# The low half of a split gelu: a VectorE subtraction, or a TensorE product and a ScalarE copy

## The chip, the cores and the metric

The kernel runs on one core of a Trainium2 chip. The metric is the device time of one execution in microseconds (us); the times shown are medians of several executions. A profile is one execution taken by the hardware profiler, and its times are counted from the first instruction of the span.

## What is computed

The input x is 8 batches of 512 tokens of width 256. Four blocks follow one another, each added to x: attention A (16 heads, attention within each token over the 64 channels of a head), a feed-forward block, attention B (causal, over the 512 tokens), and the same feed-forward block again. The part that the change touches is the feed-forward block, FFN for short:

```
def _L0_ffn_ref(x, w1_w, w1_s, w2_w, w2_s, h1_w, h1_s, h2_w, h2_s, w3_w, w3_s):
    def _tlin(x, w, s):
        return jnp.einsum('bsi,oi->bso', x, w) * s
    h = jax.nn.silu(_tlin(x, w1_w, w1_s)) * _tlin(x, w2_w, w2_s)
    h = jax.nn.gelu(_tlin(h, h1_w, h1_s), approximate=False)
    h = jax.nn.gelu(_tlin(h, h2_w, h2_s), approximate=False)
    return _tlin(h, w3_w, w3_s)
...
x = x + _L0_attn_a_ref(_layernorm(x, axis=-1), ...)
x = x + _L0_ffn_ref(_layernorm(x, axis=-1), ...)
x = x + _L0_attn_b_ref(_layernorm(x, axis=-1), ...)
x = x + _L0_ffn_ref(_layernorm(x, axis=-1), ...)
```

The hidden width is 1024, and w1, w2, h1, h2 and w3 are ternary (-1, 0, 1) with a scale for each output. The layers h1 and h2 are called the first and the second inner layer here.

## The kernel before

The kernel has two halves that run at the same time. One is attention A, in the class `AttentionA`: 8 batches, 4 groups of heads, 4 tiles of 128 tokens, 4 units of scores each. The other is the generator `after_a`: for each batch whose attention A is done, the FFN, attention B and the FFN again. So while attention A works on batch b+1, the rest of batch b runs beside it. A loop at the end of `fast_path` weaves the two by hand: each step of attention A is given out in three parts, and after each part the generator is advanced until the budget it yields (`yield 0.225 * len(step)` and so on, 309.5 a batch) has caught up. The engines' programs are then in the order in which the Python code issued them[...]. Nothing is reordered by a scheduler: an instruction that waits holds up all that stands behind it on its engine.

Attention A of one group needs all engines: TensorE projects q, k and v (L761, L766), ScalarE copies k (L781, L782), GpSimd and VectorE multiply the scores (L804), ScalarE takes the exponentials (L818), VectorE multiplies them by v (L828), a DMA that GpSimd issues adds one half of the tile to the other (L834), GpSimd folds it once more (L839), VectorE sums the rows (L865), and GpSimd adds the sums up (L872). After the last batch's attention A only the generator is left.

In the FFN, TensorE multiplies with float32r operands. Since these are rounded, an activation h is kept as two tiles: `h(0, m)`, the rounded value, and `h(1, m)`, what the rounding lost; `m` counts the 8 blocks of 128 hidden units. Each product is made twice, once with each half, and summed in PSUM. The first inner layer makes its two halves so: TensorE makes the product `pj` (L1140, one PSUM bank of 128 x 512); ScalarE writes gelu of it, rounded, to `h(0, m)` (L1105), and once more, not rounded, back over `pj` in PSUM (L1107); VectorE writes `pj - h(0, m)`, rounded, to `h(1, m)` (L1111).

The second inner layer keeps only one full float32 value, so L1107 and L1111 run for the first layer alone: 8 of each in each of the 16 FFNs.

When each of these is issued is set by the list `pending`: `later(fn)` puts a function there, and `flush()` runs and empties what the list held when it was called. The inner layers go over pairs of blocks, `m0` = 0, 2, 4, 6. The 32 products of a pair are issued in four steps of eight (three steps of 12, 12 and 8 for `m0` = 0), with a flush after each step but the last. The gelus of a pair are put on the list when its last step is out; they are issued at the flush after the first step of the next pair, and what they put on the list (`low`) at the flush after that pair's second step. The PSUM pool `ps_f` that holds `pj` has five buffers, and so a pair's bank comes free when `low` has read it.

Of the kernel before, what the change touches and what calls it, by code (L numbers as in the profile page):

```python
# [10 lines left out]
F32R = mybir.dt.float32r  # L11
BF16 = mybir.dt.bfloat16
AF = mybir.ActivationFunctionType
ALU = mybir.AluOpType
AX = mybir.AxisListType

P = 128
# [267 lines left out]
def fast_path(ctx: ExitStack, tc: tile.TileContext, k, t, flag):  # L285

    nc = tc.nc
    ident = k.ident

    const = ctx.enter_context(tc.tile_pool(name="const", bufs=1))  # L290
# [206 lines left out]
    for x1 in xn1:  # L497
        nc.gpsimd.memset(x1, 1.0)
    turn = [0]


    bank = ps_a.tile([P, 2, GW], F32, name="bank")
# [412 lines left out]
    def later(fn):  # L915
        pending.append(fn)
# [98 lines left out]
    def chunks(name):  # L1015


        pairs = {}

        def part(p, m):  # L1020
            if m // 2 not in pairs:
                pairs[m // 2] = block(f"{name}_{m // 2}", F32R).rearrange("p (n m s) -> p n m s", n=2, m=2)
            return pairs[m // 2][:, p, m % 2]

        return part
# [8 lines left out]
    def ffn(u, b, xt, nx, after):  # L1034
# [8 lines left out]
        h = chunks(f"h0_{u}")  # L1043
# [58 lines left out]
        def gelus(layer, ms, pss, h):  # L1102
            for m, pj in zip(ms, pss):
                scale = s_sb[:, 2 + layer, m : m + 1]
                nc.scalar.activation(h(0, m), pj, AF.Gelu, scale=scale)  # L1105
                if layer == 0:
                    nc.scalar.activation(pj, pj, AF.Gelu, scale=scale)  # L1107

            def low():
                for m, pj in zip(ms, pss):  # L1110
                    nc.vector.tensor_tensor(h(1, m), pj, h(0, m), ALU.subtract)  # L1111

            if layer == 0:
                later(low)

        for layer in range(2):
            h_in = h
            if layer == 0:
                h = chunks(f"h1_{u}")
            else:  # L1120
                h2 = [block(f"h2_{u}_{j}") for j in range(2)]
                h = lambda p, m: h2[m // 4][:, m % 4 * S :][:, :S]
            for m0 in range(0, MC, 2):
# [6 lines left out]
                pss = [ps_f.tile([P, S], F32, tag="pf", name=f"ph{layer}_{u}_{m}") for m in (m0, m0 + 1)]  # L1130
# [7 lines left out]
                for n, step in enumerate(steps):  # L1138
                    for j, p, c in step:
# [4 lines left out]
                            start=(p == 0 and c == 0),  # L1144
                            stop=(p == 1 and c == MC - 1),
# [5 lines left out]
                    if n < len(steps) - 1 or m0 < MC - 2:  # L1151
                        yield 0.225 * len(step)
                later(lambda layer=layer, m0=m0, pss=pss, h=h: gelus(layer, (m0, m0 + 1), pss, h))
            yield 2
            flush()
# [224 lines left out]
@with_exitstack  # L1380
def hybrid_kernel(ctx: ExitStack, tc: tile.TileContext, t):

    nc = tc.nc
    shared = ctx.enter_context(tc.tile_pool(name="shared", bufs=1))
    ident = shared.tile([P, P], F32, name="ident")
    make_identity(nc, ident)
    one = shared.tile([P, 1], F32, name="one")
    nc.gpsimd.memset(one, 1.0)
    eps = shared.tile([P, 1], F32, name="eps")
    nc.gpsimd.memset(eps, EPS)  # L1390
    power = shared.tile([P, NT], F32, name="power")
    nc.gpsimd.memset(power, -0.5)
    flag = shared.tile([P, 1], mybir.dt.int32, name="flag")

    ident16 = shared.tile([P, P], BF16, name="ident16")
    nc.vector.tensor_copy(ident16, ident)
    tmask16 = shared.tile([P, P], BF16, name="tmask16")
    nc.gpsimd.memset(tmask16, 0.0)
    nc.gpsimd.affine_select(tmask16, tmask16, [[1, P]], ALU.is_ge, NEG, base=0, channel_multiplier=-1)
    k = SimpleNamespace(ident=ident, one=one, eps=eps, power=power, ident16=ident16, tmask16=tmask16)  # L1400
    fast_path(tc, k, t, flag)
    with tc.If(nc.values_load(flag[0:1, 0:1], min_val=0, max_val=1) > 0):
        general_path(tc, k, t)
# [68 lines left out]
```

## Time and profile before

| | |
|---|---|
| time, median of 3 runs | 3989.1 us (3984.17 to 3989.51) |
| span of the profiled execution | 3990.8 us |
| mean granted TensorE clock | 0.849 |
| attention A alone (nothing beside it) | to 489 us |
| attention A beside FFNs and attention B | 489 to about 3665 us |
| last batch's FFN, attention B, FFN, alone | about 3665 to 3991 us |
| first inner layer, one pass beside attention A (14 of them) | 41.6 to 46.5 us |
| first inner layer, one pass alone (2 of them) | 29.0 us |

The span is the time from the first to the last instruction of one core. It is 1.7 us above the median of the timed runs; the profile's own sums are made against the span, and a difference found in them is taken off the median.

In the lines of the views, PE is TensorE, PEld its weight loads, DVE VectorE, ACT ScalarE, POOL GpSimd and SP the engine that issues most of the DMAs. `L1111` is a line of the kernel before. An engine's busy time doesn't count the time in which it issues a DMA, which matters for GpSimd.

### The profile page before, as it was taken

Reading aid. Unit: us, or ns where it says so; the run is one execution under the profiler, and the core shown is the slowest. Engines: PE = TensorE matmul, PEld = TensorE weight load, DVE = VectorE, ACT = ScalarE, POOL = GpSimd, SP = SyncE. Lnnn points to the kernel's source line nnn. Section 1 sums busy time; section 2 is a strip of 40 time slices with the busy share of each in tenths; the row PEclk is TensorE's granted clock in tenths of the full one; section 3 lists DMA queues with packets and bytes.
Section 4 is the critical chain, followed back from the end, with each engine's and each line's share of the span. In section 5 each row is a group of like instructions: output and inputs, shape, how many; then the busy total and the mean of one; then the engine's idle time right before and its main releaser. Section 6 shows DMA issues by size and latency. Waiting matters only on the chain.

```text
span 3990.8 us, 37932 instructions
## 1 busy us (share of the span) xinstructions
PE 3039.9 (76%) x12464; PEld 2055.2 (52%) x12464; DVE 3375.9 (85%) x3776; ACT 2341.3 (59%) x3156; POOL 3077.9 (77%) x3040
## 2 busy tenths in 40 slices
PE   5653487687877878678876878778787778778988
PEld 2231264365634656356643656346553556446847
DVE  7999988998899888998899988998989888996115
ACT  3444475576665675666755766666755767565342
POOL 6888878887888788887788887887888877886111
PEclk7556599798987988888987989879898889879999
DMA  8766777577776877768775877668776677767304
GB/s 229 182 137 137 159 197 158 124 191 189 199 154 139 196 191 178 148 163 202 200 157 118 208 186 194 149 142 213 174 190 143 160 182 206 158 129 211 116 28 169
DMA packets 118346, 669.24 MB, mean 168 GB/s; under 512 B 12662, under 2 KB 31865, under 8 KB 43643
## 3 DMA queue, kind: packets, MB, share of 16 engines
q0 software_dynamic: 78336, 570.46, 63.2%
q1 hardware_dynamic: 39804, 96.27, 6.7%
q8 instruction: 101, 1.65, 0.2%
q14 instruction: 105, 0.86, 0.1%
HBM read 254.07 MB, written 9.96 MB: 66 GB/s over the span
## 4 chain that ended last, share of the span: by engine, by line
DVE 38%; PE 18%; POOL 14%; DMA 13%; ACT 8%; issue 8%; SPq 0%; ACTq 0%; POOLq 0%; DVEq 0%
DVE red L865 15%; DMA w<-w 13%; DVE w L828 10%; PE ph L1140 5%; ACT w L818 4%; POOL w L804 3%; POOL w L839 3%; DVE ws L828 3%; PE pqkb L1187 3%; POOL acc L872 3%; DVE w L804 2%; DVE ws L804 2%; POOL h L1056 2%; POOL w L834 2%; DVE acc L876 2%
## 5 line engine op out<-in xcount | busy, mean ns | idle before, releaser
L818 ACT ACTIVATE w<-w 128x2048 f32<-128x2048 f32 x384 | 733.8, 1912 | 659.2 <-POOL w L804 461.3
L1140 PE MATMUL ph<-h,hidden 128*128 128x512 f32 x4096 | 1042.9, 411 | 72.4 <-POOL h L1056 42.9
L804 POOL TENSOR_TENSOR w<-k 128x1024 f32<-128x1024 f32 x512 | 1077.4, 2104 | 7.7 <-ACT k L782 7.1
L1140 PEld LDWEIGHTS ph<-h,hidden 128*128 128x128 f32 x4096 | 792.3, 195 | 275.3 <-POOL h L1056 53.8
L828 DVE TENSOR_TENSOR w<-w,qv 128x1024 f32<-128x1024 f32 x768 | 898.8, 1211 | 22.4 <-ACT w L818 22.4
L865 DVE TENSOR_REDUCE red<-w 128x128 f32<-128x1024 f32 (+1 forms) x384 | 601.3, 1566 | 178.0 <-DMA w<-w 93.6
L839 POOL TENSOR_TENSOR w<-w 128x1024 f32<-128x1024 f32 x256 | 643.7, 2514 | 82.9 <-DMA w<-w 82.3
L834 POOL DMA_DIRECT2D w<-w x384 | 337.9, 880 | 349.0 <-issue 121.1
L872 POOL TENSOR_TENSOR acc<-acc,red 128x256 f32<-128x256 f32 (+1 forms) x640 | 471.2, 736 | 142.7 <-DVE red L865 122.0
L865 DVE TENSOR_REDUCE red<-ws 128x256 f32<-128x2048 f32 (+1 forms) x256 | 435.4, 1742 | 0.0
L766 PE MATMUL qv<-wqv,xnta 128*128 128x512 f32 x512 | 299.7, 716 | 104.6 <-DVE ws L828 95.4
L1072 PE MATMUL pw<-xnt,gate 128*128 128x512 f32 (+2 forms) x1152 | 301.8, 422 | 21.7 <-ACT silu L1048 16.1
L828 DVE TENSOR_TENSOR ws<-ws,qv 128x1024 f32<-128x1024 f32 (+3 forms) x512 | 294.3, 635 | 27.6 <-ACT ws L818 27.6
L804 DVE TENSOR_TENSOR w<-qv,k 128x1024 f32<-128x1024 f32 x256 | 301.1, 1218 | 3.6
L804 DVE TENSOR_TENSOR ws<-qv,k 128x1024 f32<-128x1024 f32 (+3 forms) x512 | 299.5, 646 | 0.2 <-issue 0.2
L888 PE MATMUL bank<-ident,acc 128*128 128x128 f32 x256 | 62.4, 333 | 284.5 <-ACT k L781 278.6
L818 ACT ACTIVATE ws<-ws 128x1920 f32<-128x1920 f32 x128 | 231.5, 1808 | 80.7 <-DVE ws L804 80.1
L1072 PEld LDWEIGHTS pw<-xnt,gate 128*128 128x128 f32 x1152 | 230.8, 215 | 76.2 <-ACT silu L1048 20.4
L1249 ACT ACTIVATE eb<-psb 128x256 f32<-128x256 f32 (+3 forms) x512 | 182.1, 443 | 139.1 <-PE psb L1246 138.6
L1166 PE MATMUL pof<-w,h 128*128 128x256 f32 x1024 | 244.9, 392 | 22.8 <-ACT h L1105 22.8
L1105 ACT ACTIVATE h<-ph,s_sb 128x512 fp32r<-128x512 f32 (+1 forms) x256 | 171.2, 688 | 151.1 <-PE ph L1140 149.7
L876 DVE RECIPROCAL acc<-acc 128x256 f32<-128x256 f32 x128 | 222.9, 1741 | 11.9 <-POOL acc L872 11.9
(149 smaller groups left out, 4846.4 us busy)
## 6 DMA issues: line engine op xcount, KB each, us to landing
w<-w POOLq DMA_DIRECT2D x384, 1024.0 KB, 7.8
hidden<-in_h POOLq DMA_DIRECT2D x128, 1024.0 KB, 7.9
gate<-in_w12p POOLq DMA_DIRECT2D x32, 1024.0 KB, 9.1
w<-w_d SPq DMA_DIRECT2D x16, 1024.0 KB, 11.5
wqv<-wqv_d SPq DMA_DIRECT2D x31, 512.0 KB, 4.6
wo<-in_wo SPq DMA_DIRECT2D x32, 256.0 KB, 7.6
wbqk<-wbqk_d SPq DMA_DIRECT2D x8, 1024.0 KB, 9.0
w<-in_h SPq DMA_DIRECT2D x8, 1024.0 KB, 8.6
```

The lines of the kernel that those rows point to most:

```text
L766: nc.tensor.matmul(qv.rearrange("p j f -> p (j f)"), xnt[:, c, :], wqv[:, c, :], start=(c == 0), stop=(c == DC - 1),)
L804: eng.tensor_tensor(e, rows(q).to_broadcast(shape), columns(kt[:, 0]).to_broadcast(shape), ALU.mult)
L818: nc.scalar.activation(e, e, AF.Exp, scale=C**-0.5)
L828: nc.vector.tensor_tensor(ev, e, columns(qv[:, 1]).to_broadcast(list(e.shape)), ALU.mult)
L834: nc.gpsimd.dma_start(w[:, :2048], w[:, 2048:], accum_op=ALU.add)
L839: nc.gpsimd.tensor_tensor(w[:, :1024], w[:, :1024], w[:, 1024:2048], ALU.add)
L865: nc.vector.tensor_reduce(red, self.columns_of(w, n, off, nsq), AX.X, ALU.add)
L872: nc.gpsimd.tensor_tensor(rows, rows, part.rearrange("p a (x i) -> p a x i", i=n), ALU.add)
L876: nc.vector.reciprocal(acc[:, 0, :], acc[:, 0, :])
L1072: nc.tensor.matmul(pj[:, toks], w[:, m % 4, j, c, :], xs[:, p, c, toks], start=(p == 0 and c == 0), stop=(p == 1 and c == DC - 1),)
L1140: nc.tensor.matmul(pss[j], w[:, j, c, :], h_in(p, c), start=(p == 0 and c == 0), stop=(p == 1 and c == MC - 1),)
L1166: nc.tensor.matmul(po, h(0, c)[:, i * P : (i + 1) * P], w3[:, c, :], start=(c == 0), stop=False)
```

## The change

A constant tile `minus` is added: the 128 x 128 identity times -1, in float32r, made once by GpSimd. Where `low` subtracted on VectorE, a new function `less_high` now multiplies `h(0, m)` by `minus` on TensorE and adds the product onto `pj` in PSUM, so that the bank holds gelu minus its rounded copy. One flush later, ScalarE copies the bank, rounded, to `h(1, m)`. So the difference is issued on TensorE where it was on VectorE, and the tile `h(1, m)` is written one flush later, by ScalarE. The bank `pj` comes free after that copy.

```diff
--- before.py
+++ after.py
@@ -497,6 +497,8 @@
     for x1 in xn1:
         nc.gpsimd.memset(x1, 1.0)
     turn = [0]
+    minus = const.tile([P, P], F32R, name="minus")
+    nc.gpsimd.tensor_scalar(minus, ident, -1.0, None, ALU.mult)
 
 
     bank = ps_a.tile([P, 2, GW], F32, name="bank")
@@ -1106,12 +1108,17 @@
                 if layer == 0:
                     nc.scalar.activation(pj, pj, AF.Gelu, scale=scale)
 
+            def less_high():
+                for m, pj in zip(ms, pss):
+                    nc.tensor.matmul(pj, minus, h(0, m), start=False, stop=True, skip_group_check=True)
+                later(low)
+
             def low():
                 for m, pj in zip(ms, pss):
-                    nc.vector.tensor_tensor(h(1, m), pj, h(0, m), ALU.subtract)
+                    nc.scalar.copy(h(1, m), pj)
 
             if layer == 0:
-                later(low)
+                later(less_high)
 
         for layer in range(2):
             h_in = h
```

## The prediction

> **What bounds the kernel now.** I read the page's first part and chain first, then the windows of single stages, then the groups by form, and last the chain and the timeline inside two stages.
>
> ```profile
> PE 3039.9 (76%) x12464; PEld 2055.2 (52%) x12464; DVE 3375.9 (85%) x3776; ACT 2341.3 (59%) x3156; POOL 3077.9 (77%) x3040
> ...
> DVE 38%; PE 18%; POOL 14%; DMA 13%; ACT 8%; issue 8%; SPq 0%; ACTq 0%; POOLq 0%; DVEq 0%
> ```
>
> VectorE is the fullest engine and leads the chain, which speaks for taking work off it. But the change acts only in the first inner layer, so its stages decide:
>
> ```profile
> 1129.00:1223.00 94.00, 66.41 (x401) 29.25 (x399) 90.52 (x94) 60.58 (x109) 81.14 (x71) 0.88 0.70 150
> 1754.00:1799.00 45.00, 40.87 (x163) 31.30 (x162) 42.20 (x48) 37.60 (x44) 40.69 (x38) 0.94 0.86 207
> 2836.00:2879.00 43.00, 38.17 (x155) 29.78 (x155) 38.71 (x44) 34.78 (x39) 36.75 (x33) 0.96 0.84 200
> 3724.00:3753.00 29.00, 29.00 (x129) 24.02 (x128) 4.90 (x7) 10.96 (x18) 4.76 (x7) 1.00 0.43 145
> ```
>
> These are windows: length, then busy time of PE, PEld, DVE, ACT and POOL. The first is attention B beside attention A: DVE is full at 96%, the others have room. The next two are first inner layers beside attention A (a second and a first FFN of a batch): there PE, DVE and POOL are all busy for 85 to 94% of the window, and ACT has 7 to 8 us left. The fourth is one alone, all PE.
>
> The operation that goes, and its neighbours (busy time, mean ns, idle before and its releaser):
>
> ```profile
> L1055 ACT CAST h<-silu 128x512 fp32r<-128x512 f32 x128 | 78.6, 615 | 20.3 <-DVE silu L1051 19.9
> L1107 ACT ACTIVATE ph<-ph,s_sb 128x512 f32<-128x512 f32 x128 | 84.4, 659 | 0.0
> L1111 DVE TENSOR_TENSOR h<-ph,h 128x512 fp32r<-128x512 f32 x128 | 82.8, 676 | 40.0 <-ACT ph L1107 39.9
> ```
>
> The chain inside one second FFN's stage, start, length, what:
>
> ```profile
> 2696.79 0.68 DVE h L1111
> 2697.47 2.27 DVE w L804 x2
> 2699.74 0.02 issue
> 2699.77 1.92 ACT w L818
> 2701.70 1.28 ACT L1105
> ...
> 2706.03 1.50 DVE red L865 x2
> ...
> 2713.37 11.36 DMA w<-w
> ```
>
> It crosses four engines within 20 us, and L1111 holds about 1.7 us of it in a stage. Added up over the whole chain, L1111 stands there with 18 us in 49 pieces: of its 83 us, the rest lies beside other work.
>
> **What the Trainium skill says.** "TensorE: Matmul & The Clock Gate", section on the array's sub-arrays: ScalarE and VectorE are strict FIFOs. The trace agrees: L1111 sat 40 us at the head of DVE's queue until a gelu came. The same page has a warm 512-column matmul follow the last by about 216 ns; here 256 of L1140 take 58.03 us in the last stretch, 227 ns each. "ScalarE: Activation LUTs", section What ACT_TABLE_LOAD costs: 186 + 0.833 ns an element, so 612 ns for the copy, neighbours overlapping by 93; L1055 took 615, and two of them 1.12 us. Its section on table sets has copy in every set: no table load is added. "PSUM — Partial Sum Buffer", The four PSUM rules: only TensorE changes the has_written bits, so a product over a bank that ScalarE rewrote still adds to it. No run shows this yet.
>
> **The change part by part.** The built program has 128 instructions less on DVE, 128 more on PE, 128 more on ACT and one more on POOL.
>
> *Removed from DVE*: 8 x 0.676 = 5.4 us a stage. What is late next differs by stage.
> - Second FFNs beside attention A (7). At 2696 the first pair of L1111 goes, DVE's scores L804 end 1.28 us earlier, and ACT's exponential (idle 1.15 us for them) could start earlier; but two new copies, 1.12 us, now stand before it: nothing. At 2704 two L1111 and 1.2 us of waiting for gelus go, but the reduction after them needs POOL's fold L839, which ends at 2705.61: 0.4 us. At 2729 two L1111 of 1.28 us go from the chain between the landed DMA and the next issue: 1.25. In all 1.65 us, x 7 = 11.5.
> - The first FFNs of batches 0, 1 and 2 (3). The chain is POOL's up to the DMA and then passes L1111 once for 1.28 to 1.3: 3.9.
> - The first FFNs of batches 3 to 6 (4). PE runs without a gap from the late `h` of the gates, then hands to ACT:
>
> ```profile
> 2848.21 4.38 PE ph L1140 x11
> ...
> 2868.48 1.86 PE ph L1140 x8
> ...
> 2870.95 0.65 ACT ph L1107
> ...
> 2872.92 1.82 ACT ws L818
> 2874.74 0.03 issue
> 2874.76 2.35 DVE ws L828 x4
> ```
>
> Two pairs of added matmuls stand in that run, 4 x 0.227 = 0.9, with latency 1.0; at 2882.74 the chain loses 1.28 of L1111. Net 0.3 off, x 4 = 1.2.
>
> *Added to PE*: 8 x 0.227 = 1.8 us a stage. Beside attention A it lies in PE's gaps except in the four runs just counted. In the two stages of the last batch PE is at 100% (the window at 3724), so it counts whole: 2 x 1.8 = 3.6 us.
>
> *The new waits.* The added matmul waits for two gelus, with the next step's products and attention A's projections behind it on PE. Gelus are issued one step of eight (1.8 to 2.7 us) ahead of it; at 2696 they end 1.8 us before PE gets there, at 2706 2.5 us. In the first FFNs ACT itself waits for PE (2.35 us before L1105 at 2870), so PE can't overtake it. I take zero. The copy waits for the matmul, with attention A's exponentials behind it; it too is one step late, and I take its waiting as covered by ACT's idle time. The second pair is the tightest: PE would reach its matmul near 2708.4, ACT would be held from 2706.7, and the exponential at 2710.37 start 0.5 us later; its user on DVE (L828) starts only at 2715.00.
>
> *Added to ACT*: 8 copies, 4.5 us a stage, against 7 to 8 us idle. If no pair is covered, 14 x 4 x 1.12 = 63 us come on; the lower bound is zero, since ACT's gap is larger than the work. No price below zero: ACT loses nothing.
>
> *PSUM and start.* A bank is held one step longer. The second tile of the pair after next needs it, three steps later: 24 matmuls, over 5.4 us, against a copy of 1.1. Zero; if the copy is that late, PE stops. `minus` is one small POOL operation at the start, where POOL's next work waits for DVE up to 61 us: zero, at most 1 us.
>
> Sum: -11.5 - 3.9 - 1.2 + 3.6 = -13.0 us. Off the median, 3989.1 - 13.0 = 3976. The span is 1.7 us above that median, so the profile should show about 3978.
>
> **The rivals.**
> - *ScalarE becomes the late one (slower).* Each pair of copies not covered pushes the exponentials by 1.12 us, and DVE's L828 behind them. For it: 84% busy in the window at 1754, 94% with the copies, and a ring PE to ACT to PE to ACT in strict queues. Against: exponentials are mostly ready before DVE takes them. With half of the 56 pairs uncovered, 31 us against L1111's 18 and with PE's 3.6: +17, 4006. It decides from (18 - 3.6) / 1.12 = 13 pairs of 56.
> - *Hidden anyway (no change).* POOL was idle for 4.1 us before its DMA issues between 2679 and 2724, and for little else; the DMA takes 11 us whenever it starts. If POOL and the DMA take back all but a third of the gains, 5.5 off and 3.6 on: 3987.
> - *VectorE was the bound of the stage (more).* Each of the 14 shrinks until PE is full: 40.87 + 1.8 of 45 is 2.3, 38.17 + 1.8 of 43 is 3.0; mean 2.6, x 14 = 36, less 3.6: 3956. Against: POOL in the same windows.
> - That it doesn't do what it says: the counts of the program exclude it.
>
> **How the numbers follow.** Two results within 0.2% (8 us) can't be told apart here. The forecast, 3976, gets 0.46, of which 0.02 lies above 3981; more gain 0.10; hidden 0.22; slower 0.22. So faster 0.54, same 0.24, slower 0.22. The range goes from beyond the greatest gain, 3952, to the slower rival at half cover, 4004; about 2 in 10 are left out, mostly above.
>
> **What would show it.** L1111 is gone; a ScalarE row of 128 copies near 610 ns; a TensorE row of 128 matmuls. Right, if the idle time before these matmuls is small and not by ACT, if second FFNs' stages are 1 to 2 us shorter and the last stages 30.8 instead of 29.0. Wrong, if DVE's wait for ACT's L818 (50 us for w and ws before) grows by tens of us, if ACT waits long for the added matmul, or if the stages shrink by 2.5 us or more.

## The result and the profile after

The changed kernel takes 3995.1 us (median of 20 runs) against 3989.7 us of the kernel before (20 runs beside it): ratio 1.0012, interval 1.0005 to 1.0018. It is about 5 us slower, less than the 8 us that the prediction took as the least difference to be told apart; 3976 was forecast. The two profiled executions stand the other way round, 3989.3 us after and 3990.8 before. A single execution lies anywhere in a spread of some 10 us, so the traces are compared by stage and by wait here, and totals come from the timed runs.

First the page's busy times and the engines' shares of the chain, of the kernel after:

```profile
PE 3053.3 (77%) x12592; PEld 2072.2 (52%) x12592; DVE 3302.0 (83%) x3648; ACT 2400.9 (60%) x3284; POOL 3075.2 (77%) x3041
...
DVE 33%; PE 19%; POOL 17%; DMA 13%; ACT 9%; issue 8%; SPq 0%; POOLq 0%; ACTq 0%; DVEq 0%
```

VectorE gave up 73.9 us of busy time (3375.9 before) and the kernel is not faster for it. The new operations, from the groups by form (busy time, mean ns, idle before and its releaser):

```profile
L1118 ACT CAST h<-ph 128x512 fp32r<-128x512 f32 x128 | 68.4, 588 | 32.9 <-PE ph L1113 32.8
...
L1113 PE MATMUL ph<-h,minus 128*128 128x512 f32 x128 | 41.4, 397 | 3.8 <-ACT ph L1109 3.8
```

The copy costs 588 ns, close to the 612 put in, and no table load is added: ScalarE has 317 of them before and after. The matmuls' 397 ns overlap the matmuls around them (128 of them are busy for 41.4 us); what one adds is seen in the stage below.

Where the 73.9 us went is read in VectorE's waits (us in total, times, longest). The kernel before:

```profile
DVE red L865 <- DMA w<-w: 93.6, 40, 5.3
DVE red L865 <- POOL w L839: 84.1, 34, 5.7
...
DVE st L543 <- ACT x L1159: 41.1, 4, 31.3
DVE h L1111 <- ACT ph L1107: 39.9, 29, 7.3
DVE ws L828 <- ACT ws L818: 27.6, 15, 2.4
...
DVE w L828 <- ACT w L818: 22.4, 18, 2.9
```

The kernel after (its lines are 2 further down here):

```profile
DVE red L867 <- DMA w<-w: 118.0, 43, 6.2
DVE red L867 <- POOL w L841: 107.1, 50, 5.5
...
DVE st L545 <- ACT x L1166: 72.8, 4, 63.3
...
DVE ws L830 <- ACT ws L820: 47.8, 25, 4.7
DVE w L830 <- ACT w L820: 28.4, 25, 2.9
```

The row sums now wait 225.1 us for a tile that isn't there yet, 47.4 more; the products behind the exponentials wait 76.2, 26.2 more. Since the span is all but the same, the work that VectorE gave up must come back as waiting; over all rows the waits grew by about 72 us (594.9 to 666.4), and the rows show where. That these two changes make 73.6 us, almost the 73.9 us of work, is chance: the 39.9 us for L1111's gelus are gone too, and in the last batch L543 waits 31.7 us more.

The windows of the stages that the prediction showed (length, busy PE, PEld, DVE, ACT, POOL; then the granted clock), kernel after:

```profile
1751.00:1796.20 45.20, 41.69 (x170) 32.26 (x168) 38.38 (x42) 40.27 (x50) 40.72 (x38) 0.94 0.86 206
2832.80:2877.30 44.50, 39.69 (x163) 30.78 (x161) 36.40 (x39) 37.18 (x45) 37.36 (x34) 0.96 0.84 201
3718.20:3748.60 30.40, 30.40 (x135) 25.17 (x135) 0.75 (x1) 14.01 (x24) 4.79 (x7) 1.00 0.42 139
```

VectorE works 2.3 to 3.8 us less than before in the first two, and they are not shorter: 45.2 against 44.8 us and 44.5 against 43.2 from first matmul to the next stage's. GpSimd is at 40.72 of 45.20 us, where it was before. The third is the first inner layer alone: 1.4 us longer.

Over all stages, each taken from its first matmul to the first of the next (single profiled executions):

| stages | before | after | e1 |
|---|---|---|---|
| first inner layer beside attention A, 14 | 620.1 | 617.0 | 610.9 |
| second inner layer beside attention A, 13 | 574.3 | 590.1 | 593.3 |
| last layer of the FFN beside attention A, 13 | 483.4 | 467.7 | 466.6 |
| first inner layer alone, 2 | 58.0 | 60.8 | 58.0 |
| second inner layer alone, 2 | 58.0 | 59.0 | 58.0 |

The fourteenth second layer, in which attention A ends, is left out with the last layer behind it (36.9 us before, 39.8 after; 20.0 and 19.7). What the second layer loses (15.8) the last one gains (15.7): work of attention A fell to the one instead of the other (61 of the long exponentials L818 instead of 57 start in these second layers, 43 instead of 47 in the last ones). The sum of the three is -3.0, less than single executions differ by. In the last batch, where nothing runs beside, the two layers take 3.8 us more.

Last, the chain inside the second FFN's stage that the prediction showed, now from 2677.1 us (start, length, what), kernel after:

```profile
2695.71 1.05 ACT h L1118 x2
2696.76 1.82 ACT w L820
...
2703.14 1.85 PE ph L1147 x8
2704.99 0.24 PE ph L1113
2705.23 0.02 issue
2705.26 0.27 ACT h L1118
...
2705.74 0.59 ACT h L1118
...
2706.35 1.28 ACT L820
2707.63 0.01 issue
2707.64 1.93 ACT w L820
```

L1111 stood in this chain with 1.7 us. In its place stand the copies with 1.05 + 0.27 + 0.59 = 1.9 us, ahead of the exponential and of the 1.28 us in which ScalarE loads its table. The stage took 44.4 us instead of 45.0, 1.65 less was forecast. Further on, behind the landed DMA, the forecast of 1.25 us did come true. The chain from the row sum to the next issue, before:

```profile
2724.75 2.30 DVE red L865
...
2741.59 9.13 DMA w<-w
```

and after:

```profile
2721.88 2.30 DVE red L867
...
2737.53 10.86 DMA w<-w
```

That is 16.84 us before and 15.65 after.

### The profile page after: what moved, and what is told of

It reads as the page before. It is cut to its first block, busy times and chain, and to the rows that moved or that the text cites. A ratio compares the mean times of both kernels' runs of the same rounds, so it can differ in the third digit from the quotient of the medians.

```text
span 3989.3 us, 38118 instructions
## 1 busy us (share of the span) xinstructions
PE 3053.3 (77%) x12592; PEld 2072.2 (52%) x12592; DVE 3302.0 (83%) x3648; ACT 2400.9 (60%) x3284; POOL 3075.2 (77%) x3041
## 4 chain that ended last, share of the span: by engine, by line
DVE 33%; PE 19%; POOL 17%; DMA 13%; ACT 9%; issue 8%; SPq 0%; POOLq 0%; ACTq 0%; DVEq 0%
DVE red L867 14%; DMA w<-w 13%; DVE w L830 9%; PE ph L1147 5%; POOL w L806 4%; ACT w L820 4%; POOL w L841 4%; POOL acc L874 3%; PE pqkb L1194 3%; DVE ws L830 3%; DVE ws L806 2%; POOL h L1058 2%; POOL w L836 2%; DVE w L806 2%; PE pyb L1261 1%
## 5 line engine op out<-in xcount | busy, mean ns | idle before, releaser
L1173 PE MATMUL pof<-w,h 128*128 128x256 f32 x1024 | 239.2, 385 | 11.5 <-ACT h L1107 11.4
```

Source lines behind the costliest of these rows:

```text
L1173: nc.tensor.matmul(po, h(0, c)[:, i * P : (i + 1) * P], w3[:, c, :], start=(c == 0), stop=False)
```

## The experiments

Two questions: what is the subtraction worth, and what do its replacements cost? And, for the first: what hides it? Theory D says the landing of weight tiles and of the tiles to be summed, theory G says GpSimd's fold (L839). Ratios are to the kernel before, run beside on the same chip.

**The subtraction left out, nothing in its place** (e1).

```diff
-            def low():
-                for m, pj in zip(ms, pss):
-                    nc.vector.tensor_tensor(h(1, m), pj, h(0, m), ALU.subtract)
-
-            if layer == 0:
-                later(low)
...
-                            h_in(p, c),
+                            h_in(p if layer == 0 else 0, c),
```

> Leaves out the low half of the first inner layer's gelu: neither the subtraction nor anything in its place; the second inner layer multiplies the rounded half twice, so that TensorE and the two gelus on ScalarE work as before. It is the worth of the subtraction by itself. Chain theory (what the chain of waits shows of L1111 is what its removal is worth): about 17 us less than before, ratio 0.9958. Rival, GpSimd and the DMAs stand right behind VectorE: under 6 us less, ratio over 0.9985. Rival, VectorE bounds the stages: 30 us or more less, ratio 0.9925 or under.

Measured: 3983.4 us, 0.9988 (0.9981 to 0.9994). Removing the whole operation is worth 5 us (2 to 8 by the interval), not 17. VectorE's waits in this run:

```profile
DVE red L865 <- DMA w<-w: 125.8, 41, 5.5
DVE red L865 <- POOL w L839: 104.4, 49, 5.8
```

They are as long as in the changed kernel, and the two exponential waits are at 42.9 and 26.6 us. So most of the growth of VectorE's waits comes from the removal itself and not from the new operations.

**The added matmuls alone, and the copies alone** (e2 and e3).

```diff
 # e2, against e1
...
+            def less_high():
+                for m, pj in zip(ms, pss):
+                    nc.tensor.matmul(pj, minus, h(0, m), start=False, stop=True, skip_group_check=True)
+
+            if layer == 0:
+                later(less_high)
 # e3, against the changed kernel
...
             def less_high():
-                for m, pj in zip(ms, pss):
-                    nc.tensor.matmul(pj, minus, h(0, m), start=False, stop=True, skip_group_check=True)
                 later(low)
```

> As e1_no_remainder, with the added matmuls on TensorE and without the copies on ScalarE (the low half is left out, the rounded half is multiplied twice). It is the price of the added matmuls and of their wait for the gelus. Chain theory: 3.6 us above e1_no_remainder, all of it in the last batch. Rival, TensorE's wait for the gelus costs: 10 us or more above e1_no_remainder, with stages beside attention A longer than in e1.

> The changed kernel without the added matmuls: the copies on ScalarE stand at the same place and copy the bank as it is, so that the low half is a second copy of the gelu. It is the price of the copies without the wait for TensorE. Chain theory: the copies are covered, the time is that of e1_no_remainder within 3 us. Rival, ScalarE is late: 10 us or more above e1_no_remainder, with VectorE's waits for the exponentials (50 us before) grown by as much.

Measured: e2 3991.7 us, 1.0008 (1.0000 to 1.0016); e3 3980.3 us, 0.9982 (0.9973 to 0.9990). Against e1 the matmuls cost 8 us, between the two expectations, and the copies nothing (3 us less, with intervals that overlap). ScalarE does have room for 128 copies when there is no matmul for them to wait for. Both together, in the changed kernel, are 0.0024 above e1, 10 us.

**The last batch as before** (e4): the change in all batches but the last.

```diff
+            def low_dve():
+                for m, pj in zip(ms, pss):
+                    nc.vector.tensor_tensor(h(1, m), pj, h(0, m), ALU.subtract)
+
             if layer == 0:
-                later(less_high)
+                later(low_dve if b == NB - 1 else less_high)
```

> The changed kernel, but in the last batch's two FFNs the low half is made by the subtraction on VectorE as before. It separates the last batch, where TensorE is full, from the rest. If the last batch costs what the added matmuls take there (3.6 us) or what the two profiles differ by from the end of the last stage beside attention A on (5.8 us): 4 to 6 us below the changed kernel, so a ratio to before of 0.9997 to 1.0003. If the loss is all beside attention A: as the changed kernel, 1.0012.

Measured: 3987.1 us, 1.0000 (0.9992 to 1.0008). The last batch costs about 5 us of the changed kernel (1.0012 less 1.0000; the intervals just overlap, so the size is rough), and in the other seven batches the change comes out even, within 3 us.

**Half the hidden weight loads, with and without the subtraction** (e5 and e6).

```diff
-                eng.dma_start(w, src)
+                n = HB // 2 if name == "hidden" else src.shape[-1]
+                eng.dma_start(w[:, :n], src[:, :n])
...
-                            w[:, j, c, :],
+                            w[:, 0, c, :],
```

> The kernel before, with each load of hidden weights cut to its first half; the second block of each pair is multiplied with the first block's weights, and the comparison of weights covers only the half that is loaded. Theory D (the time that VectorE gave up was hidden behind the landing of weight tiles): less traffic shortens this kernel itself by 10 to 60 us, and it is only the base for the next run. Rival G (GpSimd's fold hides it): the waits of VectorE for GpSimd stay near 84 us here.

> The run e5_half_hidden_loads with the VectorE subtraction left out too (the second layer multiplies the rounded gelu twice). Theory D: with the weight tiles early, the subtraction is worth its full 17 us, so this run is at least 12 us below e5_half_hidden_loads. Rival G: it is worth about what it was worth with full loads, 5 us (3 to 8).

Measured: e5 3940.3 us, 0.9880 (0.9864 to 0.9895); e6 3931.7 us, 0.9860 (0.9845 to 0.9875). The traffic that is left out costs the kernel 47 us, and VectorE's waits for the fold are 74.0 us, near the 84 that G expected. The subtraction is worth 9 us here, just over the 3 to 8 that G expected and under the 12 of D. But the intervals overlap, and together they allow anything from nothing to some 17 us: this pair doesn't decide between D and G.

**GpSimd's fold left out, with and without the subtraction, and under the change** (e7, e8, e10).

```diff
-            nc.gpsimd.tensor_tensor(w[:, :1024], w[:, :1024], w[:, 1024:2048], ALU.add)
+            pass
```

> The kernel before, with GpSimd's fold of the tile to be reduced left out; VectorE's sum reads the first half of the tile alone, as long as before. Rival G: it shortens this kernel by 10 to 60 us and is only the base for the next run. Theory D: VectorE's 84 us of waits for the fold turn into waits for the same tiles' landing, and the time falls by less than 10 us.

> The run e7_no_gpsimd_fold with the VectorE subtraction left out too. Rival G: without the fold the subtraction is worth its full 17 us, so this run is at least 12 us below e7_no_gpsimd_fold. Theory D: 5 us (3 to 8), as with the fold.

> The changed kernel with GpSimd's fold left out, as in e7_no_gpsimd_fold. Theory G: the change takes 32 us (the subtraction, from the runs without the fold) and gives back 8 for the minus multiplications and 3 to 5 for the copies that wait for them, so it lies 17 to 26 us below e7_no_gpsimd_fold, where with the fold it lay 5 above. Rival (TensorE and ScalarE become the late ones once the fold is gone): within 8 us of e7_no_gpsimd_fold, or above it.

Measured: e7 3869.1 us, 0.9705 (0.9692 to 0.9718); e8 3837.1 us, 0.9626 (0.9613 to 0.9639); e10 3857.2 us, 0.9677 (0.9664 to 0.9690). The fold costs the kernel 118 us, far more than the 10 to 60 expected, and D's expectation fails: VectorE's waits for landing tiles don't take the place of those for the fold (80.8 us in e7, 93.6 before). Without the fold the same subtraction is worth 32 us instead of 5, more even than the 17 expected, and the change that lost 5 us gains 11 (0.9677 over 0.9705). G is confirmed in kind: with the fold there, the gain was hidden. How it hides it is not parted further: leaving the fold out takes 584 us of GpSimd's busy time away (3077.9 to 2493.5), and ScalarE's waits for GpSimd's scores fall as well (461.3 to 313.8 us before L818). Whether it is the wait for the fold itself or GpSimd's load as a whole, no run shows. It is not that the fold slows VectorE's own instructions: VectorE is busy for 3368.8 us in e7 and 3375.9 before. The expectation for e10, 17 to 26, was too high, because its cost grew as well, from 10 us to 20 (e10 over e8). Where, is seen in VectorE's waits, first e8:

```profile
DVE red L865 <- DMA w<-w: 94.4, 53, 5.3
...
DVE ws L828 <- ACT ws L818: 49.4, 23, 4.9
...
DVE w L828 <- ACT w L818: 34.4, 23, 3.6
```

and e10, the change on the same base:

```profile
DVE red L867 <- DMA w<-w: 87.4, 43, 4.5
...
DVE ws L830 <- ACT ws L820: 62.8, 25, 5.4
...
DVE w L830 <- ACT w L820: 43.1, 28, 2.9
```

The waits for exponentials go from 83.8 to 105.9 us, 22 more, where the time grows by 20; the row sums wait 7.0 less, and over all rows the waits grow by 15. This fits the first rival of the prediction, ScalarE as the late one: small until the fold is gone.

**The subtraction one flush later, still on VectorE** (e9).

```diff
             if layer == 0:
-                later(low)
+                later(lambda: later(low))
```

> The kernel before with the VectorE subtraction issued one flush of the queue of deferred work later. Theory G (what VectorE gets back goes to waits for GpSimd's fold and the landing of its tiles): the 40 us of VectorE waits for ScalarE's gelu fall below 15 us and the time moves by less than 4 us. Rival (those waits stand in the path): 10 us or more below before.

Measured: 3982.0 us, 0.9980 (0.9973 to 0.9986), 8 us better: between the two expectations. VectorE's busy time is 3376.0 us, unchanged, and its waits:

```profile
DVE red L865 <- POOL w L839: 102.7, 46, 5.6
DVE red L865 <- DMA w<-w: 79.7, 41, 5.4
...
DVE h L1111 <- ACT ph L1107: 25.3, 9, 7.2
```

All 25.3 us that are left of L1111's waiting lie in the last batch, where VectorE has time; beside attention A it fell from 15 us to nothing. So 15 us of standing at the head of a queue were worth 8 us, and taking away the work together with the standing (e1) was worth no more, 5 us; the intervals overlap, so which is more can't be said. The first expectation had asked for under 15 us in all, and had not parted the last batch from the rest.

**A quarter of the folds moved to VectorE** (e11 with the change as in e4, e12 with the subtraction as before). 64 of the 256 folds are issued on VectorE, just ahead of its sum.

```diff
-            if u == 2:
+            if u == 2 and not self.folded_late(i, u):
                 self.fold(b, i, g, u)
...
             if u == 2:
+                if self.folded_late(i, u):
+                    self.fold(b, i, g, u)
                 self.gather(b, i, g, u)
...
-            nc.gpsimd.tensor_tensor(w[:, :1024], w[:, :1024], w[:, 1024:2048], ALU.add)
+            eng = nc.vector if self.folded_late(i, n_u) else nc.gpsimd
+            eng.tensor_tensor(w[:, :1024], w[:, :1024], w[:, 1024:2048], ALU.add)
+
+        def folded_late(self, i, n_u):
+            return n_u == 2 and i % 2 == 1
```

> The run e4_last_batch_on_vector (the change in all batches but the last) with 64 of the 256 folds done by VectorE just ahead of its sum. VectorE gets 64 x 1.2 = 77 us, what the change took from it; GpSimd loses 64 x 2.5 = 161 us. Theory G: a quarter of the 118 us that the folds were worth, 20 to 30 us below before. Rival D (landing of the tiles is next in line): within 6 us of before.

> The kernel before with the same 64 folds on VectorE. Theory G: VectorE, 85% busy, takes 77 us more, of which some 32 are seen (as the same 75 us were worth without the fold), and a quarter of 118 us is saved: near before, within 15 us, and 10 us or more above e11_change_quarter_fold_on_vector. Rival D: 20 us or more above before.

Measured: e11 4035.2 us, 1.0117 (1.0102 to 1.0133); e12 4042.9 us, 1.0136 (1.0120 to 1.0151). Both are far slower. That fails both theories: e12 alone lies where D had it, but e11 lies 45 us above before, where D had expected it within 6. The row of the moved folds in e12:

```profile
L842 DVE TENSOR_TENSOR w<-w 128x1024 f32<-128x1024 f32 x64 | 131.2, 2050 | 17.8 <-DMA w<-w 17.8
```

They take 2050 ns in the mean instead of 1.2 us. The median is 1220 ns, the longest 7931. The timeline of e12 at the longest (start, length, engine, line):

```profile
825.84 7.93 DVE L842 TENSOR_TENSOR w<-w 128x1024 f32<-128x1024 f32 x1
...
826.27 2.29 POOL L806 TENSOR_TENSOR w<-k 128x1024 f32<-128x1024 f32 x1
...
828.19 0.79 POOL L878 TENSOR_TENSOR acc<-acc,red 128x128 f32<-128x128 f32 x1
...
828.61 4.06 POOL L1062 TENSOR_TENSOR h<-silu,h 128x512 fp32r<-128x512 f32 x3
```

GpSimd runs back to back to 832.67, and VectorE's fold ends 1.1 us later, about its own length. 19 of the 64 folds took over 1.6 us, and every one of them ends 1.08 to 1.20 us after the end of a GpSimd operation, nine only after two or more such operations. The Trainium skill has this on the page "SBUF — State Buffer", in its summary of rules for kernel authors: when VectorE has two SBUF inputs while GpSimd reads SBUF, "the second one to issue fully blocks until the first finishes". The trace agrees that VectorE is held up, but in those nine it is for longer than one operation. The 19 took 52 us in excess together, about the 53 that e12 lost; with the stretching in it, the test doesn't answer what the theories asked.

**The same shift with an instruction of one input** (e13, e14, e15): VectorE's sum reads those 64 tiles unfolded.

```diff
-            if u == 2:
+            if u == 2 and i % 2 == 0:
                 self.fold(b, i, g, u)
...
+                    if n_u == 2 and i % 2 == 1:
+                        both = w[:, :2048].rearrange("p (k a r j) -> p a r k j", k=2, a=2, j=JB)
+                        nc.vector.tensor_reduce(red, both, AX.XY, ALU.add)
+                    else:
+                        nc.vector.tensor_reduce(red, self.columns_of(w, n, off, nsq), AX.X, ALU.add)
```

> The kernel before without 64 of the 256 folds on GpSimd; VectorE's sum reads those tiles unfolded, 2048 values instead of 1024, an instruction of 2.28 instead of 1.21 us with one input. VectorE +68 us, GpSimd -161 us. Theory G: some 30 us saved by GpSimd (a quarter of 118) and some 30 lost on VectorE (as the 75 us of the subtraction were worth 32 without the fold): within 15 us of before. Rival P (work moved to VectorE costs whatever its kind, not by VectorE and GpSimd blocking each other): 40 us or more above, as in e12_quarter_fold_on_vector.

> The run e4_last_batch_on_vector (the change in all batches but the last) with the same 64 unfolded sums. Theory G: VectorE has the 68 us to spare here, so it is 10 us or more below e13_quarter_sum_direct, and 10 to 30 us below before. Rival P: 30 us or more above before.

> The run e9_subtract_later with the same 64 unfolded sums. Theory G: as e13_quarter_sum_direct against before, so within 15 us of e9_subtract_later and above e14_change_quarter_sum_direct. Rival P: 40 us or more above e9_subtract_later.

Measured: e13 (subtraction as before) 3980.5 us, 0.9974 (0.9966 to 0.9983); e14 (the change but for the last batch) 3974.4 us, 0.9960 (0.9946 to 0.9973); e15 (subtraction later) 3973.4 us, 0.9958 (0.9944 to 0.9972). The unfolded sums in e14:

```profile
L869 DVE TENSOR_REDUCE red<-w 128x128 f32<-128x2048 f32 x64 | 145.8, 2277 | 15.7 <-DMA w<-w 15.7
```

2277 ns in the mean, 2289 the longest. The rival P falls: with an instruction that isn't stretched, the same shift of work gains 10 us instead of losing 53. The change is 16 us below before, as G expected; that it is 6 below e13, where 10 or more was expected, says that the shift pays without it too. e15 is 9 us below e9, as expected, but not above e14: e14 and e15 beat both kernels and can't be told apart from each other.

## Why the prediction was wrong, by its own steps

**Removed from VectorE, -16.6 us: the step that failed.** Left out by itself, L1111 is worth 4.8 us (e1). In the changed kernel's stages the second FFNs moved by -1.7 us in all (309.9 to 308.2) where "1.65 us, x 7 = 11.5" stood, the first FFNs of batches 0 to 2 by -6.8 instead of -3.9, those of batches 3 to 6 by +5.4 instead of -1.2. The working asked at three places of one stage which wait comes next, found GpSimd's fold at one of them and gave that one 0.4 us, and took the 1.25 us of another whole. That piece did become 1.19 us shorter in the stage shown, in that one execution; what failed is adding such pieces up over 14 stages, as if a chain shortened inside a stage made the kernel shorter by as much. What the runs show instead is that VectorE reaches its row sums earlier and waits there for GpSimd's fold and for landing tiles (e1: 230.2 us, before 177.7). With the fold gone the same removal brings 32 us. The rival "Hidden anyway" had this right in size: all but a third taken back, 5.5 us off. Its reason that "the DMA takes 11 us whenever it starts" holds for the stages read there; over all 384 the median is 7.8 us.

**Added to TensorE, +3.6 us in the last batch.** Right: +3.8 in the four layers alone, and about 5 by e4. The stage grew by 1.4 us instead of 1.8, since the last pair's matmuls fall into the second layer, which grew by 0.5.

**The new waits, taken as zero: the second step that failed, with a smaller part of the miss.** The matmuls waited little for gelus, 3.8 us in 7 places on the row above, and 7.0 more stand before their weight loads. The copies waited 32.8 us for the matmuls, in 16 places of 128: "it too is one step late" held for most pairs. But the change costs 10 us over e1, and the last batch explains only about 5 of them, so the other 5 or so come from the matmuls and copies of the first seven batches. Which of the two, and by which wait, isn't shown. Without the fold VectorE's waits for ScalarE's exponentials grew as the time did (22 us for 20 us); with the fold they grew by 6.7 us over e1, which would fit but is near what single executions differ by. Against it stands e2, which has no copies and is 8 us above e1 all the same. The two intervals together leave about 4 to 12 us for it, so it may be little more than the last batch; this stays open.

**Added to ScalarE.** The price was right (588 ns against 612), and by itself it costs nothing that can be measured (e3).

**The sums.** Two small slips changed nothing: the mean of 2.3 and 3.0 us for the rival "more" is 2.7 and not 2.6, and the range ends at 4004 where the slower rival at half cover stands at 4006.

**What was to show it wrong.** DVE's wait for ACT's L818 grows "by tens of us": this came true, from 50.0 to 76.2. But e1 without any copy has 69.5, so the sign could not tell the slower rival from VectorE's merely arriving earlier. "If ACT waits long for the added matmul" came true too, with the 32.8 us. Of the signs for being right, the last stages did grow, to 30.4 instead of 30.8; second FFNs' stages became only 0.2 us shorter in the mean, not 1 to 2.

## What to carry to other kernels

Where several engines are each 85 to 90% busy in a stage, the fullest one's busy time is not what its work is worth: here 74 us of it were worth 5 with GpSimd's fold in place and 32 without. Before moving work off an engine, take the next one's work out as an experiment, or move some of that over at the same time (e14: -16 us, though e15, which moves nothing off VectorE, comes to -17). And look first for instructions that stand waiting at the head of a queue: issuing one later gained 8 us here, removing it 5, which is the same within the intervals. It isn't free: TensorE's weight loads then waited 8.0 us for the late halves (e9).

## What the runs showed of the hardware

A VectorE operation of two SBUF inputs, 1220 ns in the median, took up to 7931 ns in e12 while GpSimd ran without a gap, and each of the 19 stretched ones ended about one own length after the end of a GpSimd operation. Sums of one input over as many tiles stayed at 2277 ns in the mean in e14, 2289 at the longest. No run parts the number of inputs from the other ways in which the two instructions differ.
